# Two layers of adapted feed-forward networks on one core: sums of weights and tokens of the down parts moved from GpSimd to VectorE

## The chip, the core and the metric

The kernel runs on one core of a Trainium2 chip. The metric is the device time of one execution in microseconds. The engines are named as the profile names them: PE (TensorE, the matrix products; PEld is its loading of weights), DVE (VectorE), ACT (ScalarE), POOL (GpSimd) and SP (SyncE, which here only issues transfers). Each engine works through its own queue in order, and waits on semaphores for the others.

## The reference

1024 tokens (8 batches of 128) of width 512 pass through two layers. Cut to what matters here:

```python
def cond_ffn(x):                      # layer 0, first part: "c", inner width 1376
    gate, up = lora(x @ Wg.T), lora(x @ Wu.T)     # adapters of rank 16, picked by batch
    act = silu(gate) * up
    return lora_down(act @ Wd.T)                  # the "down" part
def ffn(h):                           # layer 0, second part: "f", inner width 1792
    a = h @ (gate_w * (gate_su @ gate_sv)).T      # weights times a product of rank 4
    b = h @ (up_w * (up_su @ up_sv)).T
    return (silu(a) * b) @ (down_w * (down_su @ down_sv)).T
x = x + ffn(cond_ffn(x))
x = x + ffn_int4(lora_linear(x))      # layer 1: "l", then "q" (quantised weights)
```

Everything is in fp32, in layer 0 with fp32 products.

## The kernel before

Activations lie transposed: 128 features on the partitions, the 1024 tokens along the free side in two halves of 512 (`TB`). `x` holds four such tiles of 128x1024 and is also where the result is summed; `h` is what the c part hands to the f part.

Layer 0 saves products with a Strassen-like scheme (Winograd's form): a product of 2x2 blocks is made with seven block products instead of eight, from sums and differences of weight blocks (`weight_forms`, lines 233 to 238) and of token blocks. `weight_forms` takes four blocks a11, a12, a21, a22 and makes s1 = a21 + a22, s2 = s1 - a11, s4 = a12 - s2, and overwrites a21 with a11 - a21. Its engine is an argument. It is called from two places: by `gate_up_forms` for each unit of the gate and up parts (a unit is 128 inner features; c has 11, f has 14), and by `down` for each pair of units.

`down` (lines 400 to 508) is called once for c (n = 11: five pairs and a leftover unit) and once for f (n = 14: seven pairs). What it does, in program order:

- For each pair, `weight_forms` on POOL makes a tile `ds` (128 x 3 x 256) from the two weight tiles `wd` and changes a quarter of `wd`.
- `form` (lines 420 to 427) makes one set of token differences, one 128x512 instruction a pair; the even pairs go to POOL, the odd ones to DVE. It is called four times: T3 (tile `dt`) before the products, T1 after product 1, T2 and T4 after product 3. T1, T2 and T4 are written over the activation blocks ("12", "22", "21") that they come from, so they also wait until PE has read those.
- The products come in the order 1, 2, 3, 7, 5, 6, 4, each for two halves m of the output. Products 1 and 2 read `wd` as loaded, 3, 5 and 6 read `ds`, 7 reads the changed quarter of `wd` and T3, 5 reads T1, 6 T2, 4 T4. Each is summed over the pairs in one PSUM bank; there are eight banks in turn.
- DVE and ACT take each bank out: DVE adds it to the output (lines 455, 477, 502), ACT copies it to `du` or `dv` (lines 465, 491), which POOL adds to the output (lines 467, 493, 494). With c, the hook after product 1 makes the adapters' low-rank product (`pt_d` on PE, then two DVE instructions that write `t_d`, line 201).

Products on PE are put in program order by hand (`mm`, line 70, through `in_order`). The other instructions are ordered by a scheduler, which may move them against each other unless they are wrapped in `in_order`. Before the change, the instructions of `form` are not wrapped, and of `weight_forms` only the first is.

Between the gate and up parts of f and `down` for f, the kernel issues the loads of layer 1's first weights on SP and gathers the second adapter's rows: `gather_a` (lines 156 to 181) issues five indirect transfers on POOL, and then for each of eight rows copies the slot (64 elements a partition) into `ga` and issues the next transfer into the free slot. The engine of the copies is an argument; for this gather it is DVE. The rows are used by `pt_l` at the start of layer 1. After `down` for f, POOL issues the 20 transfers of the first ten units' weights of layer q.

Of the kernel before, what the change touches and what calls it, by code (L numbers as in the profile page):

```python
# [11 lines left out]
ALU = mybir.AluOpType  # L12
# [10 lines left out]
KC = H // P  # L23
# [15 lines left out]
def kernel(  # L39
# [25 lines left out]
    nc = tc.nc  # L65

    nc_mm = nc.tensor.matmul
    in_order = tc.keep_in_program_order

    def mm(*args, **kwargs):  # L70
        in_order(nc_mm(*args, **kwargs))  # L71

    def pool(stack, name: str, side: str, bufs: int = 1):
        return stack.enter_context(
            tc.tile_pool(name=name, side=side, bufs=bufs, reuse_waits="tile")
        )
# [11 lines left out]
    def bank(name: str):  # L88
        return psum.tile([P, TB], F32, tag="bank", name=name)
# [58 lines left out]
    def gather_rows(to, table: bass.AP, rows):  # L148
        in_order(
            nc.gpsimd.indirect_dma_start(  # L150
                out=to, out_offset=None, in_=table,
                in_offset=bass.IndirectOffsetOnAxis(ap=rows, axis=0),
            )
        )

    def gather_a(pool, name: str, table: bass.AP, rows, parts, engine):


        a = [
            into.tile([P, n, NB * R], F32, tag=f"ga{i}_{name}", name=f"ga{i}_{name}")  # L160
            for i, (into, n) in enumerate(parts)
        ]
        chunks, slots = sum(n for _, n in parts), 5
        ones = []

        def gather():
            b = len(ones)
            one = pool.tile([P, chunks, R], F32, tag=f"ga1_{name}", name=f"ga1_{name}_{b}", bufs=slots)
            gather_rows(one.rearrange("p c r -> p (c r)"), table, rows[:, b : b + 1])
            ones.append(one)  # L170

        for _ in range(slots):
            gather()
        for b in range(NB):
            at = 0
            for to, (_, n) in zip(a, parts):
                in_order(engine.tensor_copy(to[:, :, bass.ts(b, R)], ones[b][:, at : at + n]))
                at += n
            if len(ones) < NB:
                gather()  # L180
        return a
# [48 lines left out]

    def weight_forms(engine, a11, a12, a21, a22, s1, s2, s4):

        in_order(engine.tensor_tensor(s1, a21, a22, ALU.add))
        engine.tensor_tensor(s2, s1, a11, ALU.subtract)
        engine.tensor_tensor(a21, a11, a21, ALU.subtract)
        engine.tensor_tensor(s4, a12, s2, ALU.subtract)  # L238

    def token_forms(pool, name: str, src, pinned: bool):  # L240

# [20 lines left out]
    def product(ps, a, b, start: bool, stop: bool):  # L262
        for n, (w, src) in enumerate(zip(a, b)):
            mm(ps, w, src, start=start and n == 0, stop=stop and n == len(b) - 1)
# [135 lines left out]
    def down(pool, layer: str, n: int, to, plus: bool, hooks, adapters=None):  # L400

        pairs = n // 2
        K2 = KC // 2
        blocks = {"11": 0, "12": 1, "21": 2, "22": 3}
        b = {
            w: [acts[2 * j + i // 2, i % 2] for j in range(pairs)] for w, i in blocks.items()
        }  # L410
        a = {i: [] for i in range(1, 8)}
        for j in range(pairs):
            wd = [ready[layer, 2 * j + i][1] for i in range(2)]
            s = pool.tile([P, 3, H // 2], F32, tag=f"ds{j}", name=f"ds_{layer}{j}")
            halves = [w[:, bass.ts(i, H // 2)] for i in range(2) for w in wd]
            weight_forms(nc.gpsimd, *halves, *(s[:, i] for i in range(3)))
            for i, w in zip((1, 2, 7, 4, 5, 6, 3), (*halves, *(s[:, i] for i in range(3)))):
                a[i].append([w[:, bass.ts(m, P)] for m in range(K2)])

        def form(t: str, x1: str, x2: str, place):  # L420
            b[t] = []
            for j in range(pairs):
                out_ = place(j)
                (nc.vector if j % 2 else nc.gpsimd).tensor_tensor(
                    out_, b[x1][j], b[x2][j], ALU.subtract
                )
                b[t].append(out_)

        def at(o: int, tb: int):
            return to[o][:, bass.ts(tb, TB)]  # L430

        banks = {}

        def sums(i: int, m: int, src: str, into=None, start=True, single=None, stop=True):


            ps = banks[i, m] = bank(f"d{i}_{layer}{m}") if into is None else into
            alone = single is not None and n % 2
            product(
                ps, [w[m] for w in a[i]], b[src], start, stop and not alone,  # L440
            )
            if alone:
                leftover(ps, m, *single, False, stop)
            return ps

        def leftover(ps, m: int, row: int, tb: int, start: bool, stop: bool):
            wd = ready[layer, n - 1][1]
            mm(ps, wd[:, bass.ts(m + 2 * row, P)], acts[n - 1, tb], start=start, stop=stop)

        def hook(i: int):  # L450
            if i in hooks:
                hooks[i]()

        def plus_bank(o: int, tb: int, ps):
            nc.vector.tensor_tensor(at(o, tb), ps, at(o, tb), ALU.add)

        def temp(what: str, m: int):
            return pool.tile([P, TB], F32, tag=f"{what}{m}", name=f"{what}_{layer}{m}")

        u = [temp("du", m) for m in range(2)]  # L460
        v = [temp("dv", m) for m in range(2)]
        more = adapters is not None
        form("T3", "22", "12", lambda j: pool.tile([P, TB], F32, tag=f"dt{j}", name=f"dt_{layer}{j}"))
        for m in range(2):
            nc.scalar.copy(u[m], sums(1, m, "11"))
            if plus:
                nc.gpsimd.tensor_tensor(at(m, 0), at(m, 0), u[m], ALU.add)
        hook(1)
        form("T1", "12", "11", lambda j: b["12"][j])
        for m in range(2):  # L470
            ps = sums(2, m, "21", None, True, (0, 0), not more)
            if more:
                extra = bank(f"d8_{layer}{m}")
                leftover(extra, m, 1, 1, True, False)
                adapters(m, [[ps, None], [None, extra]])
                nc.scalar.copy(at(m + 2, 1), extra)
            nc.vector.tensor_tensor(at(m, 0), ps, at(m, 0) if plus else u[m], ALU.add)
        for m in range(2):
            ps = sums(3, m, "22", None, True, (0, 1), not more)
            if more:  # L480
                banks[4, m] = bank(f"d4_{layer}{m}")
                adapters(m, [[None, ps], [banks[4, m], None]], {(1, 0)}, {(1, 0)})
            if plus:
                plus_bank(m, 1, ps)
            else:
                nc.scalar.copy(at(m, 1), ps)
        form("T2", "22", "T1", lambda j: b["22"][j])
        form("T4", "21", "T2", lambda j: b["21"][j])
        for m in range(2):
            ps = sums(7, m, "T3")  # L490
            nc.scalar.copy(v[m], ps)
            if plus:
                nc.gpsimd.tensor_tensor(at(m + 2, 0), at(m + 2, 0), v[m], ALU.add)
            nc.gpsimd.tensor_tensor(at(m + 2, 1), at(m + 2, 1), v[m], ALU.add)
        for m in range(2):
            ps = sums(5, m, "T1")
            plus_bank(m, 1, ps)
            plus_bank(m + 2, 1, ps)
        hook(5)
        for m in range(2):  # L500
            ps = sums(6, m, "T2")
            nc.vector.tensor_tensor(u[m], ps, u[m], ALU.add)
            for o in (m, m + 2):
                nc.vector.tensor_tensor(at(o, 1), at(o, 1), u[m], ALU.add)
            nc.vector.tensor_tensor(at(m + 2, 0), at(m + 2, 0) if plus else v[m], u[m], ALU.add)
        for m in range(2):
            ps = sums(4, m, "T4", banks.get((4, m)), not more, (1, 0))
            plus_bank(m + 2, 0, ps)


    with ExitStack() as c_layer:
# [17 lines left out]
        a1_rows, b1_rows = row_indices("1", index_tiles("1", nc.sync, idx1, idx1_rows))  # L529
# [110 lines left out]
    early = pool(ctx, "early", "left")  # L640
# [31 lines left out]
    lb = early.tile([P, KC], F32, tag="lb", name="lb")  # L672
    nc.sync.dma_start(out=lb, in_=l_b)
    b1 = gather_b(early, "1", l_bm, b1_rows, H)
    (a1,) = gather_a(early, "1", l_a, a1_rows, [(early, KC)], nc.vector)
    with ExitStack() as top:
        down(pool(top, "down_f", "right"), "f", NF, x, True, {5: turn_scales})

# [29 lines left out]
    whole, halves = slice(0, T), [bass.ts(tb, TB) for tb in range(NTB)]  # L708
# [314 lines left out]
```

## Time and profile before

| | us |
|---|---|
| median of 3 runs | 733.24 (731.67 to 737.83) |
| the profiled execution | 732.24, its span 730.5 |
| mean granted PE clock over the span | 0.99 |
| gate and up of c, with the start | 0 to 165 |
| down part of c | 164.9 to 242.1 |
| gate and up of f | 242.1 to 425.8 |
| down part of f | 425.8 to 521.5 |
| layer 1, l | 521.5 to 556 |
| layer 1, q | 556 to 730.5 |

The stages are read from PE's timeline: where its products change their operands. Busy time of each engine (us) within some of them:

| stretch | length | PE | DVE | ACT | POOL | PE clock |
|---|---|---|---|---|---|---|
| 165 to 242 | 77 | 77.0 | 28.8 | 6.0 | 33.8 | 1.00 |
| 242 to 426 | 184 | 184.0 | 90.2 | 25.8 | 73.4 | 1.00 |
| 426 to 521 | 95 | 88.4 | 28.7 | 2.3 | 61.4 | 0.95 |
| 521 to 559 | 38 | 38.0 | 7.4 | 6.2 | 1.3 | 1.00 |

In the profile's lines, the first number is the start in us from the span's start, the second the length in us; then engine, line, operation, the tiles (output<-inputs), the shape, how many in a row (x), and in brackets how long the engine was idle before and what ended that. A busy PE is not a PE at its peak, since its products are pipelined; the distance from one start to the next says more.

### The profile page before, as it was taken

The numbers are of one execution on the slowest core, as the hardware profiler recorded it, in microseconds if no ns is written. First come the engines' busy times: TensorE is split into PE (matmuls) and PEld (weight loads), VectorE is DVE, ScalarE is ACT, GpSimd is POOL, SyncE is SP. The second block draws the span as 40 slices with busy tenths as digits, with TensorE's granted clock in tenths as the row PEclk, the third lists the DMA queues.
The fourth block names the chain that finished last, engine by engine and source line by source line (L and its number), as shares of the span: only waits on it lengthen the run. The fifth ranks groups of instructions, "written<-read, shape, count | busy, mean of one in ns | idle before, by whom it ended". The sixth has DMA issues, their size and how long they took to land.

```text
span 730.5 us, 6906 instructions
## 1 busy us (share of the span) xinstructions
PE 698.1 (96%) x2526; PEld 366.3 (50%) x2526; DVE 364.8 (50%) x478; ACT 152.4 (21%) x191; POOL 380.3 (52%) x353
## 2 busy tenths in 40 slices
PE   5999999999999999999999998799999899999993
PEld 2444444444344444444444443344436687788862
DVE  4544434434035555544545360423124798899974
ACT  1111101111000111111111110000014555656552
POOL 4543524437460253443443369851301798898885
PEclk9999999999999999999999999799999999999998
DMA  8951001110020221110200020000900130000003
GB/s 303 269 190 58 29 30 57 30 30 31 0 72 1 86 59 29 41 49 29 59 5 1 15 73 0 0 29 29 373 1 9 50 86 16 15 0 1 0 1 115
DMA packets 16341, 41.48 MB, mean 57 GB/s; under 512 B 2882, under 2 KB 3162, under 8 KB 16052
## 3 DMA queue, kind: packets, MB, share of 16 engines
q1 hardware_dynamic: 10548, 25.51, 11.3%
q0 software_dynamic: 4896, 14.49, 6.2%
q10 hardware_dynamic: 864, 1.05, 0.4%
q8 instruction: 20, 0.33, 0.2%
q14 instruction: 13, 0.11, 0.0%
HBM read 37.50 MB, written 2.10 MB: 54 GB/s over the span
## 4 chain that ended last, share of the span: by engine, by line
PE 77%; POOL 11%; DMA 5%; issue 3%; ACT 1%; DVE 1%; POOLq 0%; ACTq 0%; SPq 0%; DVEq 0%
PE p_f L71 22%; PE p_c L71 17%; PE d_c L71 10%; PE gu_q L757 9%; PE d_f L71 8%; PE d_q L757 4%; PE l L722 4%; POOL sum L772 3%; PE pw L71 2%; POOL x L772 2%; POOL act_lo L772 1%; DMA wgu_c<-in_c_gu_dram 1%; DMA b<-in_idx_rows_dram 1%; DMA b_rows<-gb 1%; DMA x<-in_xT_dram 1%
## 5 line engine op out<-in xcount | busy, mean ns | idle before, releaser
L766 DVE SCALAR_TENSOR_TENSOR sum<-gu_q,sg,sum 128x1024 f32<-128x1024 f32 (+1 forms) x75 | 90.6, 1211 | 22.6 <-ACT sum L763 18.7
L757 PE MATMUL gu_q<-h_hi,wgu_q 128*128 128x512 f32 x224 | 88.8, 396 | 3.0 <-ACT sum L763 2.0
L757 PE MATMUL gu_q<-h_lo,wgu_q 128*128 128x512 f32 x224 | 87.3, 390 | 0.0
L394 POOL TENSOR_TENSOR act_f<-act_f,u_f 128x512 f32<-128x512 f32 x13 | 16.5, 1271 | 79.2 <-ACT u_f L391 79.2
L772 POOL TENSOR_TENSOR sum<-sum,sum 128x1024 f32<-128x1024 f32 (+1 forms) x15 | 33.9, 2258 | 38.7 <-DVE sum L766 38.7
L71 PE MATMUL p_f<-h,wgu_f 128*128 128x512 f32 x112 | 53.9, 603 | 0.0
L766 DVE SCALAR_TENSOR_TENSOR x<-d_q,sd,x 128x1024 f32<-128x1024 f32 (+1 forms) x49 | 53.0, 1100 | 0.9 <-PE d_q L757 0.9
L71 PE MATMUL p_f<-T_h,s_f 128*128 128x512 f32 x112 | 52.6, 592 | 0.0
L71 PE MATMUL p_f<-T_h,wgu_f 128*128 128x512 f32 x112 | 52.6, 592 | 0.0
L71 PE MATMUL p_c<-x,wgu_c 128*128 128x512 f32 x88 | 44.2, 626 | 8.3 <-DMA x<-in_xT_dram 8.3
L763 ACT ACTIVATE sum<-gu_q,sg 128x1024 f32<-128x1024 f32 (+1 forms) x45 | 47.3, 1056 | 20.0 <-PE gu_q L757 20.0
L757 PEld LDWEIGHTS gu_q<-h_hi,wgu_q 128*128 128x128 f32 x224 | 42.0, 188 | 17.3 <-ACT sum L763 3.0
L389 POOL TENSOR_TENSOR act_c<-act_c,p_c 128x512 f32<-128x512 f32 x10 | 12.8, 1277 | 70.3 <-ACT p_c L387 70.3
L757 PE MATMUL d_q<-act_hi,wd_q 128*128 128x512 f32 x112 | 44.7, 399 | 2.9 <-ACT y L763 1.6
L71 PE MATMUL d_f<-act_f,ds_f 128*128 128x512 f32 x84 | 40.2, 632 | 6.7 <-POOL ds_f L238 6.7
L757 PEld LDWEIGHTS gu_q<-h_lo,wgu_q 128*128 128x128 f32 x224 | 42.1, 188 | 8.2
L757 PE MATMUL d_q<-act_lo,wd_q 128*128 128x512 f32 x112 | 43.8, 391 | 0.8 <-POOL act_lo L772 0.8
L772 POOL TENSOR_TENSOR act_lo<-sum,act_hi 128x1024 fp32r<-128x1024 f32 (+1 forms) x15 | 33.8, 2255 | 17.8 <-ACT act_hi L833 17.8
L71 PE MATMUL p_c<-T_x,wgu_c 128*128 128x512 f32 x88 | 41.3, 592 | 0.0
L71 PE MATMUL p_c<-T_x,s_c 128*128 128x512 f32 x88 | 41.3, 592 | 0.0
L772 POOL TENSOR_TENSOR x<-x,y 128x1024 f32<-128x1024 f32 (+1 forms) x19 | 36.6, 1940 | 0.0
L71 PE MATMUL d_f<-act_f,wd_f 128*128 128x512 f32 x84 | 36.4, 592 | 0.0
(163 smaller groups left out, 1119.3 us busy)
## 6 DMA issues: line engine op xcount, KB each, us to landing
wgu_f<-in_f_gu_dram SPq DMA_DIRECT2D x14, 512.0 KB
wgu_q<-in_q_gu_dram POOLq DMA_DIRECT2D x14, 512.0 KB, 6.0
wgu_c<-in_c_gu_dram SPq DMA_DIRECT2D x10, 512.0 KB
wd_f<-in_f_down_dram SPq DMA_DIRECT2D x14, 256.0 KB
wd_q<-in_q_down_dram POOLq DMA_DIRECT2D x14, 256.0 KB
wd_c<-in_c_down_dram SPq DMA_DIRECT2D x11, 256.0 KB
out_dram<-x SPq DMA_DIRECT2D x8, 256.0 KB
b_rows<-gb SPq DMA_DIRECT2D x8, 176.0 KB
```

What stands on the lines that cost most here:

```text
L71: in_order(nc_mm(*args, **kwargs))
L389: mul(act[0], act[0], p1, ALU.mult)
L394: mul(act[1], act[1], u, ALU.mult)
L722: nc.tensor.matmul(l_sums[o][:, tb], lw[:, k, bass.ts(o, P)], x[k][:, bass.ts(tb, TB)], start=(k == 0), stop=False,)
L757: nc.tensor.matmul(ps, w, part[:, at], start=(n == 0), stop=(n == len(src) - 1))
L763: in_order(nc.scalar.activation(to, ps, AF.Identity, scale=scale))
L766: nc.vector.scalar_tensor_tensor(to, ps, scale, plus, op0=ALU.mult, op1=ALU.add)
L772: in_order(nc.gpsimd.tensor_tensor(to, a, b, op))
```

## The change

In both down parts, `weight_forms` runs on DVE in place of POOL, with all four instructions of a pair held in program order (s1, s2, s4, then a21). All token differences of `form` run on DVE, and in program order. The copies of the second gather go from DVE to POOL. What stays on POOL there: the additions onto the output, the gathers with their copies, and the transfers it issues.

```diff
-    def weight_forms(engine, a11, a12, a21, a22, s1, s2, s4):
+    def weight_forms(engine, a11, a12, a21, a22, s1, s2, s4, pinned=False):
 
         in_order(engine.tensor_tensor(s1, a21, a22, ALU.add))
-        engine.tensor_tensor(s2, s1, a11, ALU.subtract)
-        engine.tensor_tensor(a21, a11, a21, ALU.subtract)
-        engine.tensor_tensor(s4, a12, s2, ALU.subtract)
+        for to, x1, x2 in ((s2, s1, a11), (s4, a12, s2), (a21, a11, a21)):
+            made = engine.tensor_tensor(to, x1, x2, ALU.subtract)
+            if pinned:
+                in_order(made)
...
-            weight_forms(nc.gpsimd, *halves, *(s[:, i] for i in range(3)))
+            weight_forms(nc.vector, *halves, *(s[:, i] for i in range(3)), True)
...
-                (nc.vector if j % 2 else nc.gpsimd).tensor_tensor(
-                    out_, b[x1][j], b[x2][j], ALU.subtract
-                )
+                in_order(nc.vector.tensor_tensor(out_, b[x1][j], b[x2][j], ALU.subtract))
...
-    (a1,) = gather_a(early, "1", l_a, a1_rows, [(early, KC)], nc.vector)
+    (a1,) = gather_a(early, "1", l_a, a1_rows, [(early, KC)], nc.gpsimd)
```

## The prediction

> **What bounds the kernel now.** I read the busy shares first, then the chain of work that ended last, then the timeline of each engine through the two down stages.
>
> ```profile
> PE 698.1 (96%) x2526; PEld 366.3 (50%) x2526; DVE 364.8 (50%) x478; ACT 152.4 (21%) x191; POOL 380.3 (52%) x353
> PE 77%; POOL 11%; DMA 5%; issue 3%; ACT 1%; DVE 1%; POOLq 0%; ACTq 0%; SPq 0%; DVEq 0%
> ```
>
> TensorE is the bound, but 11% of the chain runs on GpSimd (POOL). Part of that is the second half of the kernel (lines 771 to 772, which the edit leaves alone). The other part lies in the second down part, which starts on PE at 425.79 us and ends at 521.48. This is the order of weight loads (PEld) there; a matmul of this type shows as two records with a load each, and PE's waits fall on the load:
>
> ```profile
> 452.40 0.19 PEld L71 LDWEIGHTS d_f<-act_f,ds_f 128*128 128x128 f32 x1 [0.24 <-issue]
> 455.37 0.30 PEld L71 LDWEIGHTS d_f<-act_f,ds_f 128*128 128x128 f32 x2 [2.78 <-POOL ds_f L238]
> 459.32 0.50 PEld L71 LDWEIGHTS d_f<-act_f,ds_f 128*128 128x128 f32 x2 [3.65 <-POOL ds_f L238]
> 463.27 0.50 PEld L71 LDWEIGHTS d_f<-act_f,ds_f 128*128 128x128 f32 x2 [3.45 <-POOL ds_f L238]
> 464.29 0.34 PEld L71 LDWEIGHTS d_f<-act_f,ds_f 128*128 128x128 f32 x1 [0.52 <-issue]
> ```
>
> The fifth, sixth and seventh pair of product 3 each wait for the last weight sum (ds_f, line 238) of that pair. The loads before are 0.43 us apart, those at 464 to 467 us are 0.85 apart: the granted clock fell too (0.54 over 456 to 464 us, 0.76 over 464 to 470). And this is why the sums are late:
>
> ```profile
> 448.06 1.25 POOL L424 TENSOR_TENSOR act_f<-act_f,act_f 128x512 f32<-128x512 f32 x1
> 449.29 0.71 POOL L236 TENSOR_TENSOR ds_f<-ds_f,wd_f 128x256 f32<-128x256 f32 x1
> 449.97 0.72 POOL L237 TENSOR_TENSOR wd_f<-wd_f 128x256 f32<-128x256 f32 x1
> 450.65 0.71 POOL L238 TENSOR_TENSOR ds_f<-wd_f,ds_f 128x256 f32<-128x256 f32 x1
> 451.33 0.71 POOL L235 TENSOR_TENSOR ds_f<-wd_f,wd_f 128x256 f32<-128x256 f32 x1
> 452.02 1.26 POOL L424 TENSOR_TENSOR act_f<-act_f,act_f 128x512 f32<-128x512 f32 x1
> ```
>
> POOL runs without a gap from 433.08 to 464.4 us, one pair every 3.95 us, with a token difference or an addition onto x between the weight sums; PE takes a pair every 0.86. DVE meanwhile is idle: its timeline has one 0.69 us addition between 437.5 and 457 us.
>
> The size of the loss: 28 records of product 3 take from 449.82 to 472.02, 22.20 us. The 28 of product 7 right after take 12.02 (472.02 to 484.04). The difference is **10.2 us**. Of it 8.7 are the waits (2.5, 3.1 and 3.1, the loads' positions against a 0.43 us step) and 1.5 the lower clock. In the first down part (164.86 to 242.12) PE's timeline shows no wait on POOL at all, so nothing is to be won there:
>
> ```profile
> 173.64 4.96 PE L71 MATMUL pt_d<-act_c,ga 128*32 128x256 f32 x88
> 178.53 6.28 PE L71 MATMUL d_c<-act_c,wd_c 128*128 128x512 f32 x14
> 184.73 1.13 PE L71 MATMUL d_c<-t_d,b_down 64*128 64x512 f32 x4
> ```
>
> [...] 0.42 (unit 0's weight sums, which DVE makes at 7.65 to 9.2 us) and 0.69. [...] here 0.73 against 0.42 and 1.27 against 0.68. [...]
>
> ```profile
> 467.11 12.66 POOL L424 TENSOR_TENSOR act_f<-act_f,act_f 128x512 f32<-128x512 f32 x8 [2.67 <-PE d_f L71]
> 467.93 9.37 DVE L424 TENSOR_TENSOR act_f<-act_f,act_f 128x512 f32<-128x512 f32 x6 [1.85 <-PE d_f L71]
> 427.78 1.88 DVE L424 TENSOR_TENSOR dt_f<-act_f,act_f 128x512 f32<-128x512 f32 x3
> ```
>
> Side by side a DVE difference costs 1.56 us, alone 0.60 (1.88 for three, less overlap). [...]
>
> **The change, part by part.** In the order of instructions as the two kernels are built, PE, ACT and SP keep theirs (one run of pt_l products is only split by a wait). POOL loses 68 rows and DVE gains 68.
>
> *Weight sums to DVE.* 28 instructions for the f part, 20 for the c part. Unit 0 shows the pace: 0.34 us from one to the next, 0.45 where the next needs the result. The new order (s1, s2, s4, a21) has two such steps, so a pair costs 0.45+0.45+0.34+0.34 = 1.58 us. For the upper end I take 0.56 each, the widest step among the contended sums at 20 to 25 us.
> f part: DVE is free at 427.86, after the last unit's product (line 389). 7 x 1.58 = 11.1, all sums ready at 438.9 (upper 443.5). The first is loaded at 449.39, the seventh pair at 449.39 + 6 x 0.86 = 454.5. Cover: 10 us, so the waits and the low clock go: **-10.2 us**.
> c part: DVE is free at 168.75. 5 x 1.58 = 7.9, to 176.7 (upper 180.0). Needed at 193.06. Nothing.
>
> *Token differences to DVE, pinned behind the sums* (0.60 each). What was in DVE's queue now stands behind them:
> - c part: T3, five, 3.0 us, to 179.7; then t_d, the masked low-rank product, which before was made at 178.66 to 179.42. Two at about 0.38: now 180.5 (upper 183.8). PE takes it up at 184.73. This is the thinnest cover of the whole change, 4 us, at the upper end 1. T1 follows to 183.5 (upper 186.8), wanted at 214.6; the additions onto h at 186 and 193 keep their place or slip by under 1 us, which only holds a PSUM bank.
> - f part: T3 to 443.1, wanted at 461.4; T1 to 447.3, wanted at 473.4. Two additions onto x of product 2 (line 477) stand behind T1, 447.3 instead of the 444.3 at which PE delivers; their banks are wanted again eight banks later, about 485.
> - T2 overwrites what product 3 reads, so it starts when PE is through (about 461.8), with T4 14 x 0.60 = 8.4, to about 471; wanted at 487 and 499. In the c part from 203.9 to 210, wanted at 223 and 232. Nothing.
>
> *The second gather's copies to POOL.* Eight copies, nearest row 0.29 us for a 128x128 copy there: at most 2.3 us. Three gather issues wait behind them as they waited for DVE's copies before. The first addition onto x (line 467) stands behind six copies, but its input comes at 432.6 and POOL has nothing else. pt_l wants the copies 80 us later. Nothing. Bound from above for DVE[...]: copies 2.3, gathers 3 x 1.0, two additions 2.5, together 8 us; even on top of the upper end the last sum is there at 451.5, before 454.5.
>
> *Queues.* POOL's 20 weight loads for the next layer stand behind its additions; before, the second waited for PE until 508.21, so they start 10 us earlier with PE and the first is used at 545.7 instead of 555.9, more than 40 us on. On SP five loads of wd_f now wait for DVE (done at 177) where they waited for POOL; PE's last read of those tiles at 242 decides as before.
>
> The sum: 732.24 (profiled execution: span 730.5 and 1.74 around it) - 10.2 = **722.1 us**. That execution lies 1.0 below the shown median; the median less 10.2 is 723.0. I put 722.5.
>
> **The rivals.**
> *The gain comes in part.* DVE and POOL get in each other's way more than bounded, or t_d comes late. For: the 1.56 us instructions above. Against: POOL has 8 us of work beside DVE's burst where it had 31. At half the gain, 727.
> *The gain is given back later*, at the start of the quantised layer, where POOL and DVE chains hold PE (559 to 605 us). Against: all that feeds it is released by PE or lies 30 us ahead. 732.
> *DVE becomes the bound (slower).* Place: the same two stages. With d us per weight sum, t_d is late in the c part by 20d + 172.5 - 184.7 and the last f sum by 27d + 427.9 - 454.5: together 47d - 39 where both are positive. It eats the 10.2 from d = 1.04. At 1.25 it is 9.7 us net, 742. For: beside POOL, DVE's differences slowed 2.6 times, and 2.6 x 0.42 is 1.09. Against: that took a POOL as dense as DVE, and POOL is nearly empty then.
> That the scheduler undoes the move is excluded by the built order.
>
> **How the numbers follow.** Full gain 0.80 (722.5, own range 720.5 to 725.5: the runs before lie 0.6 below to 5.6 above the profiled one, their median 1.0 above), part 0.08, given back 0.06, slower 0.06. About 1% (under 725.9 or over 740.6) is what a measurement can tell from no change. Faster: 0.80; same: most of the second and third, 0.14; slower: 0.06. Range 720 to 727: the full and the partial gain; the other two, 0.12, are left out.
>
> **What would show it.** In PE's timeline product 3 of the f part runs 28 records in 12 us at full clock, and nobody waits for ds_f; the down part takes 85.5 us instead of 95.7. The f sums sit on DVE at about 1.6 us a pair, done near 439. In the c part PE passes 184.73 with no wait for t_d. The next layer starts 10 us earlier and takes the same 209 us. A PE wait on DVE for ds, dt or t_d, or a wait for wgu_q at 546, would prove me wrong.

## The result, and the profile after

The changed kernel takes 724.21 us (median of 4 runs, 720.86 to 728.11), the kernel before 733.94 on the same chip (4 runs, 731.67 to 737.83). The ratio is 0.9869, 95% interval 0.9838 to 0.9899: faster by 1.3%. Run again later beside another set of runs of before it took 722.71, ratio 0.9842 (0.9810 to 0.9873). The forecast was 722.5 us with a range of 720 to 727; one of the first four runs, 728.11, lies outside it.

The page of the kernel after, its busy shares and its chain of waits; they answer to the two lines shown of before:

```profile
PE 697.6 (96%) x2526; PEld 367.5 (51%) x2526; DVE 388.5 (53%) x546; ACT 152.4 (21%) x191; POOL 311.4 (43%) x285
PE 88%; POOL 5%; DMA 4%; ACT 1%; DVE 1%; issue 1%; POOLq 0%; ACTq 0%; DVEq 0%
```

POOL gave up 69 us of work (380.3 to 311.4) for which DVE needs 24 (364.8 to 388.5). POOL's share of the chain falls from 11% to 5%; nearly all that remains of it is in layer 1. PE's busy time is almost the same in both pages and says little about the gain: in the f part it falls from 89.0 to 85.5 us, while it is busy 3.0 us longer in the start and in layer 1, at a mean granted clock of 0.98 where before had 1.00 and 0.99.

The f down part, PE's timeline of after (start, length, idle before in brackets if there was any):

```profile
430.52 24.20 PE L71 MATMUL d_f<-act_f,wd_f 128*128 128x512 f32 x56
454.56 12.18 PE L71 MATMUL d_f<-act_f,ds_f 128*128 128x512 f32 x28
466.57 12.18 PE L71 MATMUL d_f<-dt_f,wd_f 128*128 128x512 f32 x28
```

Product 3 is now one line of 28 records from 454.56 to 466.57, 12.01 us, as long as product 7 behind it. Before it took 22.20 us in pieces. The loads of its fifth to seventh pair, where the waits of 2.8 to 3.7 us stood, are as far apart as all the others:

```profile
457.99 0.19 PEld L71 LDWEIGHTS d_f<-act_f,ds_f 128*128 128x128 f32 x1 [0.24 <-issue]
458.42 0.19 PEld L71 LDWEIGHTS d_f<-act_f,ds_f 128*128 128x128 f32 x1 [0.24 <-issue]
458.85 0.19 PEld L71 LDWEIGHTS d_f<-act_f,ds_f 128*128 128x128 f32 x1 [0.24 <-issue]
459.28 0.19 PEld L71 LDWEIGHTS d_f<-act_f,ds_f 128*128 128x128 f32 x1 [0.24 <-issue]
```

What supplies them is DVE's timeline in the same part:

```profile
432.27 0.47 DVE L235 TENSOR_TENSOR ds_f<-wd_f,wd_f 128x256 f32<-128x256 f32 x1
...
443.58 1.37 DVE L237 TENSOR_TENSOR ds_f<-ds_f,wd_f 128x256 f32<-128x256 f32 x1
444.99 0.42 DVE L237 TENSOR_TENSOR ds_f<-wd_f,ds_f 128x256 f32<-128x256 f32 x1
445.33 0.42 DVE L237 TENSOR_TENSOR wd_f<-wd_f 128x256 f32<-128x256 f32 x1
445.67 4.29 DVE L425 TENSOR_TENSOR dt_f<-act_f,act_f 128x512 f32<-128x512 f32 x7
449.88 4.29 DVE L425 TENSOR_TENSOR act_f<-act_f,act_f 128x512 f32<-128x512 f32 x7
```

The seven pairs take 13.4 us, the last sum that PE waits for (s4) is there at 445.4, and PE loads it at 459.3: 13.9 us ahead. One sum took 1.37 us in place of 0.42; POOL's addition onto x runs from 443.41 for 1.27 us beside it. The same happens once more at 437.8.

**Where the time went.** Stage by stage, from PE's timelines: the f down part went from 95.69 to 85.51 us, that is 10.18 less. The c down part is 77.26 and 77.25. Yet the two profiled spans differ by only 4.1 us (730.5 and 726.4). Two other terms stand against the 10.18. The profiled execution of after began its c down part 4.74 us later (169.60 against 164.86), and its layer 1 took about 1.3 us longer (210.37 us against 209.02). Both are followed up below.

### The profile page after: what moved, and what is told of

Its sections match the earlier page's. It is cut to its first block, busy times and chain, and to the rows that moved or that the text cites. A ratio compares the mean times of both kernels' runs of the same rounds, so it can differ in the third digit from the quotient of the medians.

```text
span 726.4 us, 6900 instructions
## 1 busy us (share of the span) xinstructions
PE 697.6 (96%) x2526; PEld 367.5 (51%) x2526; DVE 388.5 (53%) x546; ACT 152.4 (21%) x191; POOL 311.4 (43%) x285
## 4 chain that ended last, share of the span: by engine, by line
PE 88%; POOL 5%; DMA 4%; ACT 1%; DVE 1%; issue 1%; POOLq 0%; ACTq 0%; DVEq 0%
PE p_f L71 23%; PE p_c L71 18%; PE d_f L71 12%; PE gu_q L756 12%; PE d_c L71 10%; PE d_q L756 5%; PE l L721 4%; DMA ga<-in_c_a_dram,a_rows 3%; PE pw L71 2%; POOL sum L771 2%; POOL x L771 1%; POOL act_lo L771 1%; DMA b<-in_idx_rows_dram 1%; PE pt_d L71 1%; PE l L71 1%
## 5 line engine op out<-in xcount | busy, mean ns | idle before, releaser
L390 POOL TENSOR_TENSOR act_c<-act_c,p_c 128x512 f32<-128x512 f32 x10 | 12.7, 1274 | 72.4 <-ACT p_c L388 72.4
L771 POOL TENSOR_TENSOR act_lo<-sum,act_hi 128x1024 fp32r<-128x1024 f32 (+1 forms) x15 | 33.8, 2254 | 18.8 <-ACT act_hi L832 18.8
L71 PE MATMUL d_f<-act_f,ds_f 128*128 128x512 f32 x84 | 36.6, 593 | 0.0
```

The costliest lines, as they stand in the source:

```text
L390: mul(act[0], act[0], p1, ALU.mult)
L771: in_order(nc.gpsimd.tensor_tensor(to, a, b, op))
```

## The experiments

State of the question: theory A is the prediction's, that PE waited because one POOL queue held 31 us of work while DVE idled. Theory B says that DVE and POOL shut each other out while both work (a difference took DVE 1.56 us beside POOL's and 0.60 alone), so that only a move of everything pays. Theory C says that the fixed order does it. Theory D says that DVE is now nearly the bound itself. The lengths of the down parts come from each run's own profile, the medians and ratios from 4 to 20 runs. The runs of before differ from set to set (medians 733.8 to 736.4 us), so the medians of different rows are only roughly comparable.

| run | f part us | c part us | median us | ratio to before (95%) |
|---|---|---|---|---|
| before | 95.69 | 77.26 | 733.94 | |
| after | 85.51 | 77.25 | 724.21 | 0.9869 (0.9838 to 0.9899) |
| f part alone | 85.51 | 77.26 | 722.06 | 0.9799 (0.9741 to 0.9856) |
| c part alone | 97.52 | 77.25 | 734.84 | 0.9998 (0.9975 to 1.0021) |
| weight sums alone | 86.85 | 78.40 | 724.80 | 0.9877 (0.9819 to 0.9935) |
| token differences alone | 90.89 | 77.26 | 726.54 | 0.9878 (0.9848 to 0.9907) |
| order left open | 85.51 | 77.26 | 722.45 | 0.9818 (0.9787 to 0.9850) |
| copies on DVE | 85.51 | 77.25 | 723.62 | 0.9839 (0.9803 to 0.9875) |
| first sum six times | 88.33 | 77.26 | 727.18 | 0.9860 (0.9799 to 0.9920) |
| first sum eleven times | 106.42 | 83.17 | 750.85 | 1.0198 (1.0138 to 1.0257) |
| after, again | 85.51 | 77.25 | 722.71 | 0.9842 (0.9810 to 0.9873) |
| loads later | 85.51 | 77.26 | 722.06 | 0.9833 (0.9805 to 0.9861) |

### The f part alone, and the c part alone

```diff
-            weight_forms(nc.vector, *halves, *(s[:, i] for i in range(3)), True)
+            on_dve = layer == "f"
+            weight_forms(
+                nc.vector if on_dve else nc.gpsimd, *halves, *(s[:, i] for i in range(3)), on_dve
+            )
...
-                in_order(nc.vector.tensor_tensor(out_, b[x1][j], b[x2][j], ALU.subtract))
+                made = (nc.vector if layer == "f" or j % 2 else nc.gpsimd).tensor_tensor(
+                    out_, b[x1][j], b[x2][j], ALU.subtract
+                )
+                if layer == "f":
+                    in_order(made)
```

For the c part alone "f" becomes "c", and the second gather's copies go back to DVE.

> The change in the f down part alone; the c down part is as before. Theory A (all of the gain is the f part's waits): f down part 85.5 us, c down part 77.3, ratio 0.987. Rival (the c part gave something too, or took something): ratio differs from the whole change's 0.9869 by more than 0.003.

> The change in the c down part alone; the f part and the second gather's copies are as before. Theory A: nothing gained and nothing lost, c down part 77.3 us, f down part 95.7, ratio 1.000. Rival: t_d stands behind the sums on DVE, PE waits for it and the c part gets longer than 77.6.

The stages came out as theory A has it: the f part holds all of the gain (85.51 us, as in the whole change), and the c part neither gives nor takes (77.25 and 77.26; ratio of the c part alone 0.9998). The ratio of the f part alone, 0.9799, differs from the whole change's 0.9869 by more than the 0.003 that the rival had named. But its interval is wide and its own c part is unchanged, so the stages don't bear that rival out. In the run of the c part alone the f part is built as before, yet takes 97.52 us and not 95.69. PE's timeline there shows why:

```profile
455.95 1.98 PE L71 MATMUL d_f<-act_f,ds_f 128*128 128x512 f32 x2 [2.66 <-POOL ds_f L237]
459.89 2.08 PE L71 MATMUL d_f<-act_f,ds_f 128*128 128x512 f32 x2 [1.96 <-POOL ds_f L237]
463.84 10.04 PE L71 MATMUL d_f<-act_f,ds_f 128*128 128x512 f32 x16 [1.87 <-POOL ds_f L237]
473.72 1.45 PE L71 MATMUL d_f<-dt_f,wd_f 128*128 128x512 f32 x3
```

The waits end at the same 3.95 us rhythm of POOL. Of the 1.83 us more, 0.7 come before: the fifth pair follows the start of product 3 (449.70) after 6.25 us, in the profile of before after 5.55. The other 1.1 come behind the waits: the last 16 records take 9.9 us to the next line, where the same 16 took 8.75 in before (463.27 to 472.02). At product 7's 0.43 us a record they would take 6.9: the pace was low in both, and for longer here. The mean granted clock of the whole span is 0.985 here and 0.990 there; a part of that difference lies in layer 1, where 10 us were granted 0.83 here and 1.00 there. So the same row of waits costs 10.2 us in one execution and 12.0 in another.

### Half of the move: weight sums alone, token differences alone

Weight sums alone: `form` as before, the copies back on DVE. Token differences alone: `weight_forms` as before (POOL, not held in order), the copies back on DVE.

> Only the weight sums of both down parts go to DVE, in fixed order; the token differences stay shared between DVE and POOL and the second gather's copies stay on DVE. Theory A (PE waited only because one POOL queue held all the weight sums, half the token differences and two additions, 31 us of work, while DVE idled): the f down part falls from 95.7 to about 85.5 us, ratio about 0.987, as with the whole change. Theory B[...]: POOL still has T3, T1 and two additions, some 12 us beside the sums; if each shuts DVE out, the last sum is ready at 458 to 460 instead of 454.5 and 3 to 5 us of the 10.2 stay lost. Theory C (the order of the token differences has to be fixed): the gain is missing or partial although no sum waits on POOL.

> Only the token differences go to DVE, in fixed order; the weight sums stay on POOL, the second gather's copies on DVE. Theory A: POOL then makes a pair of sums in 2.75 us instead of 3.95, and starts earlier, near 431.5 us because the last gathers no longer wait for DVE's queue; the last sum at 451 to 453, wanted at 454.5, so the f down part takes about 85.5 to 86. Theory B[...]: the 14 differences that DVE makes meanwhile, 8.4 us, push the sums by up to that, the last at 460, PE loses up to 5 us plus a part for the clock: f down part 88 to 92 us, ratio 0.990 to 0.996. The c part keeps its 77.3 us either way.

Theory B has a part in both, though with the weight sums alone less is lost than the 3 to 5 us that it expected. With the token differences alone, theory A expected about 85.5 to 86 and theory B 88 to 92; it is 90.89, so only 4.8 of the 10.2 us are won. POOL's timeline of that run:

```profile
432.50 0.72 POOL L237 TENSOR_TENSOR ds_f<-wd_f,ds_f 128x256 f32<-128x256 f32 x1
433.19 1.17 POOL L235 TENSOR_TENSOR ds_f<-wd_f,wd_f 128x256 f32<-128x256 f32 x1
...
448.43 1.17 POOL L235 TENSOR_TENSOR ds_f<-wd_f,wd_f 128x256 f32<-128x256 f32 x1
449.68 0.72 POOL L237 TENSOR_TENSOR ds_f<-ds_f,wd_f 128x256 f32<-128x256 f32 x1
```

From 432.5 to 449 us, exactly as long as DVE makes its 14 differences, most sums on POOL take 1.17 us in place of 0.72. The differences suffer too: seven take 8.59 us there, 4.29 in the kernel after. The last sum is ready at 457.5, which is 458.5 on the time scale of before (the f part begins 1.0 us earlier here): far behind theory A's 451 to 453 and near theory B's 460 at the latest.

With the weight sums alone the f part loses only 1.3 us and the c part 1.1. What is late in the f part is the start of the sums. DVE's timeline, with POOL's beside it:

```profile
437.35 8.41 DVE L177 COPY ga<-ga 128x64 f32<-128x64 f32 x1 [2.22 <-DMA ga<-in_l_a_dram,a_rows]
445.68 0.41 DVE L235 TENSOR_TENSOR ds_f<-wd_f,wd_f 128x256 f32<-128x256 f32 x1
```

```profile
435.88 2.49 POOL L425 TENSOR_TENSOR dt_f<-act_f,act_f 128x512 f32<-128x512 f32 x2
438.32 1.26 POOL L468 TENSOR_TENSOR x<-x,du_f 128x512 f32<-128x512 f32 x1
439.55 4.93 POOL L425 TENSOR_TENSOR act_f<-act_f,act_f 128x512 f32<-128x512 f32 x4
444.44 1.26 POOL L468 TENSOR_TENSOR x<-x,du_f 128x512 f32<-128x512 f32 x1
```

A copy of 64 elements, 0.18 us elsewhere in this timeline, stands in DVE for 8.41 us and ends as POOL's unbroken row of instructions ends, at 445.7. All 28 sums wait behind it. This is also what the copies' move to POOL guards against, though the next run shows that it isn't needed once POOL has no such row. In the c part the mix of both engines' work delays t_d, and PE waits for it 1.07 us at 185.1.

The timed ratio of the token differences alone (0.9878) is lower than its stages explain: 4.8 us are 0.65%. Its profiled span less the begin of its c part is 561.0 us against 565.6 of before, which agrees with the stages. The runs of before that it is compared with have a median of 736.39, 2.4 us above the first set. Those runs of before have no trace, so where they lost the rest stays open. The stages, not the ratios, decide between half and whole.

### The order left open, and the copies on DVE

Order left open: `weight_forms` without its last argument `True`, `form` without `in_order`. Copies on DVE: only `gather_a` gets `nc.vector` again.

> The whole change without the fixed order: everything of the changed kernel on DVE, but the token differences and three of the four sums of a pair are left to the scheduler, which puts a T3 difference into each pair of sums. Theory A: a pair then costs 1.58 + 0.60 = 2.2 us on DVE, seven 15.3, the last sum near 447.5 of the time scale of before, wanted at 454.5; no wait, f down part 85.5 us, ratio 0.987. Theory C (order needed): a wait for ds or a longer down part shows, above 86.5 us.

> The whole change, except that the second gather's eight copies stay on DVE. They are in program order ahead of the f part's sums, so DVE's queue waits for the gathers' transfers before it starts on them. Theory A: the copies end near 434 to 437 instead of 428 on the time scale of before, the last sum near 446 to 450 (cover to 454.5), so still no wait of PE: f down part 85.5 us, ratio 0.987; the move of the copies is worth nothing. Rival (thin cover): PE waits for the sums, f down part 87 or more.

Both keep 85.51 and 77.26 us: theory C falls, and the copies' move is worth nothing by itself. On DVE the copies hold back the sums to 434.1 us, and the last sum that PE waits for is ready at 445.9, still some 9 us ahead of its load.

### How much cover DVE has left

```diff
-        in_order(engine.tensor_tensor(s1, a21, a22, ALU.add))
+        for _ in range(1 + 5 * pinned):
+            in_order(engine.tensor_tensor(s1, a21, a22, ALU.add))
```

The second run has 10 for 5.

> The whole change with the first sum of each pair made six times instead of once, the same values again: five additional DVE instructions a pair, 1.7 to 2.25 us (0.34 to 0.45 each). Theory A, by the prediction's formula with what the changed kernel's trace shows (t_d ready 4.3 us ahead of PE in the c part, the last f sum about 13.9 us ahead of its load): c down part longer by 5 x 1.7 to 2.25 less 4.3, that is 4.2 to 7 us; f part by 0 to 2 us, since 7 x 1.7 to 2.25 is 12 to 15.8. Together 4 to 9 us over the changed kernel, ratio to before 0.992 to 0.999. Rival D (DVE already the bound): the whole 20 to 27 us of added work shows, ratio over 1.01. Rival (cover larger, nothing waits): ratio 0.987.

> As the run with six, but the first sum of each pair made eleven times: ten additional DVE instructions a pair, 3.4 to 4.5 us. Theory A: c down part longer by 5 x 3.4 to 4.5 less 4.3, 12.7 to 18.2 us; f part by 7 x 3.4 to 4.5 less 13.9, 9.9 to 17.6 us, and some more for PE's clock after the waits. Together 23 to 38 us over the changed kernel, slower than before: ratio 1.018 to 1.04. Rival D (no cover at all): 41 to 54 us, ratio over 1.04.

A repeated sum costs 0.46 us, a little over the 0.34 to 0.45 expected, so a pair takes 3.89 and 6.19 us. The f part grew by 2.82 and 20.91 us, more than expected (0 to 2; 9.9 to 17.6), the c part by 0 and 5.92, less than expected (4.2 to 7; 12.7 to 18.2). Together 2.8 us, below the 4 to 9 expected, and 26.8, inside the 23 to 38, but there by two errors of opposite sign.

The c part: the expectation took over the prediction's step that t_d stands behind all sums and T3 on DVE. DVE's timeline of the run with eleven shows another order:

```profile
182.34 0.42 DVE L236 TENSOR_TENSOR ds_c<-wd_c,wd_c 128x256 f32<-128x256 f32 x1
182.67 0.42 DVE L201 TENSOR_TENSOR t_d<-pt_d,mask 128x256 f32<-128x256 f32 x1
183.00 0.42 DVE L236 TENSOR_TENSOR ds_c<-wd_c,wd_c 128x256 f32<-128x256 f32 x1
183.34 0.42 DVE L201 TENSOR_TENSOR t_d<-pt_d,mask 128x256 f32<-128x256 f32 x1
183.67 4.09 DVE L236 TENSOR_TENSOR ds_c<-wd_c,wd_c 128x256 f32<-128x256 f32 x9
```

t_d is not pinned, and the scheduler put it among the sums when those grew. What PE then waited for was a sum itself, at 202. The f part with eleven: the additions onto x slipped in the same way between the sums (0.7 us each), and two sums took 1.37 us in place of 0.42, as the two beside POOL's additions did in the kernel after. PE's last 16 records behind the waits took 9.1 us (480.75 to 489.89), with six 7.0 (459.83 to 466.81); the mean granted clock of the span is 0.979 with eleven and 0.994 with six.

Theory D falls: the five repeats a pair add 27.6 us of work (12 pairs of 5 sums of 0.46 us), and 2.8 of it show. The kernel after has room on DVE of about 2 us a pair in the f part, and then pays in full.

### The start, and a version with loads moved

```diff
-            nc.sync.dma_start(out=wgu, in_=c_gu[f])
+            made = nc.sync.dma_start(out=wgu, in_=c_gu[f])
+            if f > 3:
+                in_order(made)
...
-        nc.sync.dma_start(out=ready["c", f][1], in_=c_down[f])
+        in_order(nc.sync.dma_start(out=ready["c", f][1], in_=c_down[f]))
...
         load_c(1)
-        load_c_down(0)
...
                 arrange_b()
+                load_c_down(0)
```

The eight transfers of `arrange_b` are wrapped in `in_order` too.

> The changed kernel once more, beside the run below on the same chip. If the 4.7 us by which its profiled execution began the first down part later (169.6 against 164.9 us) are chance of the start (the first gather's rows landed late, PE idled 3.2 us at 32 to 35 us and its clock fell), this profile begins that part at 163.5 to 166 and its span is about 720.5; if they belong to the change, it begins it at 169 again and the span is near 726.

> The changed kernel with two transfers of the start moved in SP's queue behind the eight copies of the adapter rows (b_rows): the first down weights and the fifth unit's gate and up weights, 0.75 MB that are wanted much later. The transfer engines are full from 8 to 38 us and the first gather's rows are among what they carry. If those 0.75 MB, 2 to 2.5 us at 300 to 390 GB/s, delay the gather, PE's second half of pt_gu starts at 31.5 to 32 us instead of 32 to 35 and the kernel is 1 to 3 us faster than the changed one, and varies less. If the gather is limited by its own issue on POOL, it starts as before and nothing changes.

The changed kernel's second profile begins the c part at 166.10, just outside the 163.5 to 166 expected of chance and far from the 169 expected if the change caused it; its span is 722.9 us. The nine profiles of before and of the eight runs up to here, in which nothing of the start is edited, begin it anywhere from 163.83 to 167.01. So the start differs from execution to execution, and nothing ties it to the change. In the first profile of after PE's timeline reads:

```profile
29.56 2.35 PE L71 MATMUL pt_gu<-x,ga 128*32 128x256 f32 x36
35.12 3.06 PE L71 MATMUL pt_gu<-x,ga 128*32 128x256 f32 x28 [3.21 <-POOL ga L177]
38.97 2.16 PE L71 MATMUL p_c<-t_gu,b_rows 32*128 32x256 f32 x16 [0.79 <-DVE t_gu L566]
```

The second 28 products wait for the last gathered rows. With two loads moved behind, the same place reads:

```profile
29.65 3.66 PE L71 MATMUL pt_gu<-x,ga 128*32 128x256 f32 x64
34.12 1.21 PE L71 MATMUL p_c<-t_gu,b_rows 32*128 32x256 f32 x16 [0.81 <-DVE t_gu L567]
```

No wait, and the c part begins at 163.07, the earliest of all profiles. But that does not show that the moved loads removed the wait: four profiles without this edit, the changed kernel's second among them, have the same unbroken row of 64, and in the others apart from the first of after the wait is 0.96 us at most. Its six runs lie between 721.71 and 722.43, those of the changed kernel beside it between 721.41 and 725.43. The medians are 722.06 and 722.71: the 1 to 3 us expected did not come, and one can't be called faster than the other (the ratios' intervals overlap almost wholly). That it varies less is what six runs each show; why is open.

## Why the prediction was right

- **The size.** The step "22.20 less 12.02" gave 10.2 us, and the f part is shorter by 10.18; 85.51 us is the 85.5 forecast. This was right because all of it stood in one row of one stage. That it fits to hundredths says less than it seems to. The wait was priced from the very profile that it is compared with, and the run of the c part alone shows the same row of waits at 12.0 us. Of the 10.2, the part for the low clock (1.5 us by the prediction) was that execution's own.
- **Weight sums on DVE.** 1.58 us a pair was forecast; in the c part, where POOL is idle, a pair takes 1.59 (173.48 to 175.07). In the f part seven took 13.4 us and not 11.1, inside the upper end of 15.7: two of them lost about a microsecond to POOL's additions onto x. That left the last sum 13.9 us ahead of its load, where the prediction's own times give 15.6, and 11.0 at its upper end.
- **Token differences, and t_d.** T3 and T1 took 4.2 us each, as forecast. t_d was ready at 185.19 and taken at 189.47, 4.3 us ahead where 4 had been counted. But the prediction read as a rule ("what was in DVE's queue now stands behind them") what was only the scheduler's choice in this build. The runs with repeated sums showed it to move t_d when that gets late. The forecast doesn't suffer from it; the slower rival's formula does, which for the c part counts a wait of t_d: with 6.19 us a pair it gives 18.8 us there, measured were 5.9.
- **The slower rival.** Its other half held in kind: with sums of 1.55 us each (6.19 a pair) the formula gives 34 us in all and the run lost 26.8, slower than before. The f part lost more than its term (20.9 against 15.3 us), the c part much less. That DVE does not get there by itself was right.
- **Part of the gain, by two engines in each other's way.** Given 0.08. It did not come in the whole change, since POOL was busy for only 5.5 us beside DVE's 13.4 us of sums; it is what happens when only half is moved. The prediction's bound of 8 us let DVE stand still for the whole of POOL's work; the sums lost 2.3 us (13.4 against 11.1).
- **Given back later.** The step "takes the same 209 us" was off by 1.3 us. The wait that is there is the same in both, 2.01 and 2.00 us for ACT at the start of layer q. PE's clock behind it is not. Before:

```profile
577.12 0.50 PE L757 MATMUL gu_q<-h_hi,wgu_q 128*128 128x512 f32 x1 [2.01 <-ACT sum L763]
577.45 0.39 PE L757 MATMUL gu_q<-h_lo,wgu_q 128*128 128x512 f32 x1
577.68 0.40 PE L757 MATMUL gu_q<-h_hi,wgu_q 128*128 128x512 f32 x1
```

After:

```profile
571.61 0.80 PE L756 MATMUL gu_q<-h_hi,wgu_q 128*128 128x512 f32 x1 [2.00 <-ACT sum L762]
572.20 0.63 PE L756 MATMUL gu_q<-h_lo,wgu_q 128*128 128x512 f32 x1
572.63 0.63 PE L756 MATMUL gu_q<-h_hi,wgu_q 128*128 128x512 f32 x1
```

Records 0.43 us apart in place of 0.23, for some eight of them. In both profiles every change of the granted clock lies on a grid of 3.41 us steps. In before the changes come at 456.64, 466.88 and 726.29 us, 3 and 76 steps apart; in after at 35.75, 42.58, 571.64, 575.05 and 721.83, 2, 155, 1 and 43 apart. Against the span's start the two grids lie about 1 us apart. In after, the whole pause lies in one step (568.23 to 571.64 us, PE busy for 1.23 us of it), and the next step is granted 0.50 of the clock. In before, the grid cuts the same pause in two (572.69 to 576.10 and on to 579.52, PE busy for 2.23 and 2.40 us), and the clock stays at 1.00.

Of the twelve profiles, eight have layer 1 at 210.3 to 210.7 us and four at 209.0 to 209.2. Over 10 us with this pause and what follows it, the mean granted clock is 0.83 in the eight and 1.00 in the four. The c part alone, whose f part is that of before, is among the eight; both runs with repeated sums, which are the changed kernel with more work, are among the four. So nothing ties the 1.3 us to the change. That the place of the pause on the grid decides is what the profiles of before and after suggest; for the other ten it was not shown.

- **The median.** 722.5 was set between the two anchors; 724.21 and, repeated, 722.71 were measured. The profiled run of the first set, 728.11, has the late start and these 1.3 us in it; its other three runs have no trace.

## What to carry to other kernels

Read a stage's loss as the difference of two rows that do equal work, one that waits and one that doesn't; the stage gained just that here. The difference includes the slower pace behind a wait, and that part varies from execution to execution (the same 16 records took 8.75 us in one and 9.9 in another). When two engines share a burst of work and slow each other (here DVE's seven differences took 8.59 us beside POOL's sums and 4.29 without them), moving half of it can win less than half (4.8 of 10.2 us) or move the wait elsewhere (to the copy of 8.41 us); move the whole burst to the faster one if its queue has room (a sum took 0.42 us on DVE, 0.72 on POOL). Say of an instruction that stands behind others whether it is pinned there: a scheduler may move it, and then another wait is the one to price.

## What the runs showed of the hardware

The prediction's pairs of times are those of a sum of two tensors in the kernel before: 128x256 takes 0.42 us on DVE and 0.73 on POOL, 128x512 takes 0.68 to 0.69 on DVE and 1.27 on POOL.

Side by side both engines took longer here. In the kernel before, six differences of DVE beside eight of POOL took 1.56 us each, and POOL's 1.58. With the token differences alone, seven differences beside POOL's sums took 8.00 us, 1.14 for one of each, where 0.60 and 0.69 alone make 1.29: nearly the sum of both, and a little under it.

A copy of 64 elements on DVE (weight sums alone) stood for 8.41 us beside an unbroken row of POOL's two-input instructions, and ended with the row. No instruction of the row took longer than 1.26 us, and six of them began meanwhile. That it is a copy does not decide this alone. In the kernel before, one that began at 436.83 us was done after 0.72, as POOL's instruction under way ended, although POOL's next followed without a gap. What decides stays open.

The granted clock of PE went to half for one 3.41 us step after a pause of 2.0 us that lay wholly in the step before, and stayed at 1.00 where the grid cut such a pause in two with PE busy for 2.23 and 2.40 us of the steps (see "Given back later"). In two other places it was at half for longer: two steps (35.75 to 42.58 us of after) behind the wait of 3.21 us for gathered rows, and three (456.64 to 466.88 us of before) in the row of waits for POOL's sums.
